# Stores on ScalarE's queue, later turns and a last item summed by quarter, in the last product of a layer on one core

## The chip, the cores and the metric

The kernel runs on one core of a Trainium2 chip. The metric is the time of one execution on the device in microseconds (us). The core has a matrix engine (TensorE, PE in the profile, with its weight loads as PEld), three engines for elementwise work (VectorE is DVE, ScalarE is ACT, GpSimd is POOL), and SyncE (SP), which here only starts transfers. Each engine works through its own instructions in order. A transfer (DMA) is started by an instruction in the queue of one of these engines, and such an instruction waits, like any other, until what it needs is ready; what is behind it on that engine waits too.

## What is computed

The inputs are 4 sequences of 512 tokens with 1024 features, all in float32.

```python
xn = layernorm(x)                                     # x: (4, 512, 1024)
qkv = xn @ w_qkv                                      # 32 query heads, 8 key/value heads of 128
scores = einsum('bqhgd,bkhd->bhgqk', q, k) * scale
attn = softmax(scores - slopes * sqrt(distance), causal)
a = einsum('bhgqk,bkhd->bqhgd', attn, v).reshape(4, 512, 4096)
out = x + a @ w_o + (xn @ W.T + b) + lora(xn)         # lora: one of four ranks per token
```

The last line is one product in the kernel: the 1024 features of xn and the 4096 of a are contracted together (5120 rows of weights, W above w_o), and the low-rank term and the bias come in as a further product over 65 rows. Its result is 2048 tokens by 1024 features, to which x is added.

## The kernel before

**Stages.** A first stage normalises x and projects it to q, k and v (to about 1150 us of the profiled execution), a second one does the attention (to about 1880 us), and the function finish does the last product (from about 1950 us to the end). Only finish is touched.

**The last product.** It is done with seven products in place of eight at each of three levels (the Winograd form of Strassen's scheme). The outer level is the index i, taken in the order OUTER = (1, 2, 6, 5, 3, 7, 4); the middle level is m, in the order MIDDLE = (1, 2, 3, 6, 7, 4, 5); one pair (i, m) is an item, and there are 49 items. The inner level is class Inner: seven products of five matmuls each (KB = 5 blocks of 128 rows; 128x128 weights against 256 tokens), in seven methods m1, m5, m6, m3, m2, m7, m4. Results stand transposed, features on partitions and tokens along them.

**The loop.** The loop at the end of finish runs an item's methods and calls beside(n, slot) after each, with slots 1 to 7; the method m4 of the item before (prev.m4) runs between slots 2 and 3. So a slot, or step, is one inner product on TensorE. In beside stand the operand sums of the next item, tokens(k) on VectorE and weights(k) on GpSimd, and the loads of the item after next (L1167 for tokens, tiles sa; L1173 to L1182 for weights, tile w). All are in a fixed order on their engines: the calls are wrapped in pin, which keeps program order, and TensorE's order is the program's.

**PSUM and its readers.** Each inner product lands in a bank of the kinds c, d or a. Where an item has a base (a tile that its result is added to), VectorE reads the bank (L128, tiles m, x, u and the like). Where it has none, which are the items with m = 1 or m = 5 and two with m = 3, ScalarE copies it (L166). The accumulation that follows in the same bank waits for that read.

**Sums and stores.** When an item's last quarter is there, after(row, col) adds whole tiles of 128x1024 elements, mostly on GpSimd, and calls done(at, t) of class Outer. What done does depends on i. For i = 1, 6 and 5 the tile goes to a scratch tensor c_d named u, w or v, with a store on SP's queue (L1387), and is loaded again later (taken, L1367) as the base of a later i. For i = 7 GpSimd adds the tile to y and v; y is stored on SP's queue (L1393), and v is a result and leaves. For i = 2, 3 and 4 the tile is a result and leaves.

**Leaving.** leave(t, where) loads the matching rows of x into a tile x_t (L1346, SP's queue, two transfers of 256 KB) and appends two turns to the queue leaving, one for each pair of sequences p. A turn does four transposes on TensorE (L1352, tile ptr_f), adds x on VectorE (128x512) and stores the result on SP's queue (L1355). A slot of 5 or later takes one turn from the queue. The x tile has four buffers, so a load of x rows waits for the store that used its buffer before.

**The end.** The last item is (4, 5). Its after adds the whole tile x_5 to y for the quarter (0, 1) on VectorE, then u and y to it on GpSimd for the quarter (1, 1); each sum leaves in two turns, which are emptied after the loop.

Of the kernel before, what the change touches and what calls it, by code (L numbers as in the profile page):

```python
# [65 lines left out]
def kernel(  # L66
# [13 lines left out]
    nc = tc.nc  # L80
# [5 lines left out]
    NP = B // 2  # L86
# [5 lines left out]
    xf = x.rearrange("b (t p) h -> p (b t) h", p=P)  # L92
    outf = out.rearrange("b (t p) h -> p (b t) h", p=P)
# [16 lines left out]
    def scratch(name, shape):  # L110
        return dram.tile(shape, F32, tag=name, name=name)
# [10 lines left out]
    c_d = {  # L122
        (n, r, c): scratch(f"c{n}_{r}{c}", [P, 2, NP, HS])
        for n in ("u", "w", "v", "y") for r in range(2) for c in range(2)
    }

    def add(eng, dst, u, v):
        return eng.tensor_tensor(dst, u, v, ALU.add)  # L128
# [1020 lines left out]
    order = [(i, m) for i in OUTER for m in MIDDLE]  # L1149
    pin = tc.keep_in_program_order  # L1150
# [126 lines left out]
    def finish(sb, homes, ops, begun):  # L1277
        bank_of = rotation(c=(3, 0), d=(2, 4), a=(5, 1), tr=(6, 7))

        def bank(kind, name):  # L1280
            t = bank_of(kind, name)
            return t if kind == "tr" else t[:, :HS]
# [4 lines left out]
        def r4(name, tag="r4"):  # L1287
            return sb.tile([P, 2, NP, HS], F32, tag=tag, name=name, bufs={"r4": 8, "u": 2}[tag])

        def quarter(t, row, col):  # L1290
            return t[:, col, row]
# [12 lines left out]
        def of(n):  # L1304
            if n not in ops:
                ops[n] = Operands(n, homes)
            return ops[n]
# [25 lines left out]
                pin(sub(nc.gpsimd, w[:, :, 2], w[:, :, 0], w[:, :, 1]))  # L1333


        leaving = deque()

        def rows(t, p, row, col, r, c):
            at = (2 * p + row) * NT + 2 * r
            return t[:, at : at + 2, ds(col * S + c * HS, HS)]  # L1340

        def leave(t, where):
            n = "_".join(str(k) for k in where)
            x_t = sb.tile([P, NP, 2, HS], F32, tag="x", name=f"x_{n}", bufs=4)
            for p in range(NP):
                nc.sync.dma_start(out=x_t[:, p], in_=rows(xf, p, *where))  # L1346

            def turn(p):
                tr = bank("tr", f"f_{n}_{p}").rearrange("p (a b k) -> p a b k", a=2, b=2)
                for k in range(2):  # L1350
                    for j in range(2):
                        nc.tensor.transpose(tr[:, k, j], t[:, j, p, ts(k, P)], ident)  # L1352
                y = x_t[:, p].rearrange("p a (b k) -> p a b k", b=2)
                pin(add(nc.vector, y, tr, y))
                nc.sync.dma_start(out=rows(outf, p, *where), in_=x_t[:, p])  # L1355

            for p in range(NP):
                leaving.append(lambda p=p: turn(p))


        BASE = {2: "u", 6: "u", 5: "w", 3: "v", 4: "y"}
        KEPT = {1: "u", 6: "w", 5: "v"}
        PLACE = {2: (0, 0), 3: (0, 1), 4: (1, 0)}
# [6 lines left out]
        class Outer:  # L1370
# [13 lines left out]
            def done(self, at, t):  # L1384
                i = self.i
                if i in KEPT:
                    pin(nc.sync.dma_start(out=c_d[(KEPT[i], *at)], in_=t))  # L1387
                elif i in PLACE:
                    leave(t, (*PLACE[i], *at))
                else:  # L1390
                    y, v = self.given.pop(at)
                    pin(add(nc.gpsimd, y, y, t))
                    pin(nc.sync.dma_start(out=c_d[("y", *at)], in_=y))  # L1393
                    pin(add(nc.gpsimd, v, v, t))
                    leave(v, (1, 1, *at))

        def item(n, outer):
            i, m = order[n]
            name = f"{i}_{m}"
            o = ops[n]  # L1400
            t = outer.t
            has = outer.base is not None
            base = None
            if m == 1:
                dst = t["u"] = r4(f"u_{i}", "u")
            elif m in (6, 7):
                dst = base = t["u"]
            elif m == 3 and has:
                dst = base = outer.given.pop((0, 1))
            else:  # L1410
                dst = r4(f"x_{name}")
                if m in (2, 4):
                    base = t["u"]
            t[m] = dst
            left = [4]

            def after(row, col):
                left[0] -= 1
                if left[0]:
                    return  # L1420
                if m in (2, 4):
                    at = {2: (0, 0), 4: (1, 0)}[m]
                    if has:
                        pin(add(nc.gpsimd, dst, dst, outer.given.pop(at)))
                    outer.done(at, dst)
                elif m == 6:
                    pin(add(nc.gpsimd, t[3], t[3], dst))
                elif m == 5:
                    pin(add(nc.vector, t[3], t[3], dst))
                    outer.done((0, 1), t[3])  # L1430
                    pin(add(nc.gpsimd, dst, dst, t["u"]))
                    if has:
                        pin(add(nc.gpsimd, dst, dst, outer.given.pop((1, 1))))
                    outer.done((1, 1), dst)

            def into(row, col):
                return quarter(dst, row, col)

            def base_of(row, col):
                return quarter(base, row, col)  # L1440

            if n == 0:
                return Plain(name, bank, o, into, None, after, begun)

            def mult(l, bk, start):
                if i in RANKED and m in RANKED and l in RANKED:
                    (_, _), (r, c), (p, d) = RANKED[i], RANKED[m], RANKED[l]
                    nc.tensor.matmul(
                        bk, low["w"][:, c, d], low["u"][:, p, ts(r, HS)], start=start, stop=False,
                        skip_group_check=True,  # L1450
                    )
                    start = False
                for _ in o.steps(l, bk, start):
                    pass

            return Inner(name, bank, tmp, mult, into, base_of if base is not None else None, after)

        def beside(n, slot):

            if n + 1 < len(order):  # L1460
                nxt = of(n + 1)
                {1: lambda: n and (nxt.tokens(1), nxt.weights(1)), 2: lambda: (nxt.tokens(2), n and nxt.weights(2)),
                 3: lambda: nxt.weights(3), 4: lambda: (nxt.tokens(4), nxt.weights(4)),
                 5: lambda: nxt.tokens(3)}.get(slot, lambda: None)()
            if n + 2 < len(order):
                o = of(n + 2)
                {2: lambda: o.load(1, 0), 3: lambda: (o.load(1, 1), o.load_weights()),
                 4: lambda: o.load(0, 0), 6: lambda: o.load(0, 1)}.get(slot, lambda: None)()
            if leaving and slot >= 5:
                leaving.popleft()()  # L1470

        outers = {}
        prev = None
        for n, (i, m) in enumerate(order):
            if m == 1:
                outers[i] = Outer(i)
                if i in RANKED:
                    low_rank(i)
            if n + 1 < len(order) and order[n + 1][1] != 1:
                outers[i].prefetch(order[n + 1][1])  # L1480
            it = item(n, outers[i])
            it.m1()
            beside(n, 1)
            it.m5()
            beside(n, 2)
            if prev is not None:
                prev.m4()
            beside(n, 3)
            for slot, step in ((4, it.m6), (5, it.m3), (6, it.m2), (7, it.m7)):
                step()  # L1490
                beside(n, slot)
            prev = it
        prev.m4()
        while leaving:
            leaving.popleft()()

    psum = ctx.enter_context(pool("psum", space=bass.MemoryType.PSUM))
    homes, begun = [], {}
# [41 lines left out]
    with tc.manual_schedule(engines={PE}):  # L1540
        with pool("c1") as home:
            homes.append(home)
            lay(home, "x")
            next(attention, None)
            with pool("c2") as sb:
                homes.append(sb)
                finish(sb, homes, ops, begun)
# [35 lines left out]
```

## Time and profile before

| what | value |
|---|---|
| median of 3 runs | 2747.62 us (2742.18 to 2752.84) |
| the profiled execution's own time | 2745.72 us |
| its span, first to last instruction | 2743.9 us |
| busy in the span: PE, DVE, ACT, POOL | 2623.8, 1772.3, 651.2, 1939.4 us |
| last product, 1952 to 2744 us: PE, DVE, ACT, POOL busy | 764.4, 473.3, 22.8, 475.6 us of 792 |
| DMA in the last product | 0.78 of the 16 engines, 275 GB/s |
| x rows, issue to landing | 5.5 / 6.7 / 10.9 us (min, median, max; 32 loads) |
| output stores, issue to landing | 2.2 / 3.8 / 5.4 us (32 stores) |
| scratch stores, issue to landing | 2.9 / 3.0 / 3.0 us |

How to read it. The times are those of one profiled execution. Busy time leaves out the instructions that issue transfers; they are listed as SPq or ACTq, the engine's sequencer. PE, DVE and the others overlap, so an idle engine costs nothing unless TensorE, or the end of the kernel, waits for it. DMA share is the mean busy share of the core's 16 DMA engines. L128, L131 and L166 are lines of small helpers (add, sub, Inner.read), so groups are told apart by the names of their tiles: t<-w are weight sums, s<-sa token sums, x, u, v, w and y result tiles.

### The profile page before, as it was taken

To read this page: it belongs to the slowest core of one execution; us is meant where nothing else is said; L and a number is where in the kernel's file an instruction comes from. 1 tells how busy PE (TensorE), PEld (TensorE's weight loads), DVE (VectorE), ACT (ScalarE), POOL (GpSimd) and SP (SyncE) were. 2 spreads that over 40 slices of the span, in tenths; PEclk is the share of its full clock that TensorE was granted. 3 is DMA by queue.
4 is the path that set the end of the run, shared out by engine and by line. 5 is a ranking of instruction groups with operands and counts; after the bars stand their busy time and mean duration, and the time that the engine had idled before them with its cause. 6 is when DMAs were issued, how large, how long until landed. Compare 5 with 4: busy or idle time off the path is not lost.

```text
span 2743.9 us, 35857 instructions
## 1 busy us (share of the span) xinstructions
PE 2623.8 (96%) x11872; PEld 2089.3 (76%) x11872; DVE 1772.3 (65%) x3620; ACT 651.2 (24%) x1727; POOL 1939.4 (71%) x1999
## 2 busy tenths in 40 slices
PE   7899999997999999999999999998799999999998
PEld 6688888886888888866666666666688888888887
DVE  6766675666667667566666666675456667566553
ACT  3001111100000000176666666663000000000000
POOL 2688877887898888667777777776465667656563
PEclk9899999999999999999999999999899999999999
DMA  3289776754966767326666666767788878788883
GB/s 135 85 297 339 258 247 203 268 186 157 345 230 232 255 216 249 138 101 217 203 218 202 219 202 220 245 220 247 271 287 308 295 289 328 234 299 302 295 292 114
DMA packets 377098, 648.06 MB, mean 236 GB/s; under 512 B 22057, under 2 KB 280489, under 8 KB 367698
## 3 DMA queue, kind: packets, MB, share of 16 engines
q1 hardware_dynamic: 324594, 583.51, 61.7%
q10 hardware_dynamic: 51040, 57.68, 6.7%
q0 software_dynamic: 1280, 4.59, 0.4%
q8 instruction: 95, 1.56, 0.2%
q14 instruction: 89, 0.73, 0.1%
HBM read 387.74 MB, written 257.96 MB: 235 GB/s over the span
## 4 chain that ended last, share of the span: by engine, by line
PE 60%; DMA 6%; POOL 4%; DVE 3%; issue 2%; SPq 0%; POOLq 0%; ACT 0%; ACTq 0%; DVEq 0%
PE pc L1228 12%; PE psc L980 10%; PE po L1018 10%; PE pc_q L549 6%; PE pd L1228 5%; PE ptr L1005 3%; PE pd_q L549 3%; PE pa L1228 3%; PE pc_kv L549 3%; DMA sa<-s 1%; PE pa_q L549 1%; PE pd_kv L549 1%; DMA w<-in_w_o_dram 1%; DMA s<-ot 1%; DVE pt L1008 1%
## 5 line engine op out<-in xcount | busy, mean ns | idle before, releaser
L994 POOL TENSOR_SCALAR p<-p,tot 128x256 f32<-128x256 f32 (+3 forms) x512 | 317.9, 642 | 134.4 <-DVE tot L992 81.3
L985 DVE CUSTOM_DVE_ANT_0 p<-psc,bias 128x256 f32<-128x256 f32 (+3 forms) x512 | 245.1, 491 | 95.6 <-PE psc L980 72.6
L980 PE MATMUL psc<-k,q 128*128 128x512 f32 (+3 forms) x1024 | 305.3, 437 | 1.3 <-ACT r_q L166 0.5
L989 ACT ACTIVATE p<-p,low 128x256 f32<-128x256 f32 (+3 forms) x512 | 283.8, 555 | 71.0 <-DVE low L985 53.6
L131 POOL TENSOR_TENSOR t<-w 128x640 f32<-128x640 f32 x96 | 181.9, 1895 | 154.6 <-DMA w<-m 62.6
L1018 PE MATMUL po<-pt,v 128*128 128x512 f32 x640 | 290.6, 592 | 0.0
L980 PEld LDWEIGHTS psc<-k,q 128*128 128x128 f32 x1024 | 172.8, 190 | 99.6 <-issue 55.5
L131 POOL TENSOR_TENSOR t<-w,t 128x640 f32<-128x640 f32 x96 | 199.4, 2077 | 51.5 <-PE pc L1228 47.7
L1005 PEld LDWEIGHTS ptr<-ident,p 128*128 128x128 f32 x1280 | 147.3, 141 | 73.2 <-issue 39.4
L1018 PEld LDWEIGHTS po<-pt,v 128*128 128x128 f32 x640 | 116.8, 190 | 108.5 <-issue 99.3
L549 PE MATMUL pc_q<-x,ti_q 128*128 128x256 f32 x704 | 182.7, 382 | 11.0 <-DVE u_q L128 5.8
L131 POOL TENSOR_TENSOR wr<-wr 128x256 f32<-128x256 f32 x220 | 170.0, 775 | 25.9 <-DMA wr<-in_w_o_dram 9.7
L1008 DVE COPY pt<-ptr 128x512 f32<-128x512 f32 x192 | 129.9, 683 | 82.0 <-PE ptr L1005 80.2
L1005 PE MATMUL ptr<-ident,p 128*128 128x128 f32 x1280 | 167.7, 274 | 6.1 <-DVE pt L1008 4.7
L549 PE MATMUL pc_q<-xi,ti_q 128*128 128x256 f32 x640 | 167.8, 385 | 3.4 <-DVE q L128 2.9
L131 POOL TENSOR_TENSOR ti_q<-w_q 128x256 f32<-128x256 f32 x128 | 106.0, 828 | 86.0 <-PE pc_kv L549 45.7
L549 PEld LDWEIGHTS pc_q<-x,ti_q 128*128 128x128 f32 x704 | 133.2, 191 | 32.9 <-DVE u_q L128 7.5
L166 ACT COPY m<-pc 128x256 f32<-128x256 f32 x30 | 11.2, 372 | 594.5 <-PE pc L1228 586.3
L131 DVE TENSOR_TENSOR wr<-wr 128x256 f32<-128x256 f32 x220 | 139.0, 632 | 11.5 <-DMA wr<-in_w_o_dram 5.9
L549 PEld LDWEIGHTS pc_q<-xi,ti_q 128*128 128x128 f32 x640 | 121.0, 192 | 24.7 <-issue 5.9
L549 PE MATMUL pd_q<-xi,ti_q 128*128 128x256 f32 x448 | 116.6, 383 | 4.2 <-POOL ti_q L131 4.2
L166 ACT COPY q<-pc_q 128x256 f32<-128x256 f32 x64 | 23.8, 373 | 386.7 <-PE pc_q L549 342.1
(300 smaller groups left out, 5947.7 us busy)
## 6 DMA issues: line engine op xcount, KB each, us to landing
sa<-s SPq DMA_DIRECT2D x98, 640.0 KB, 7.7
s<-ot SPq DMA_DIRECT2D x107, 384.0 KB, 3.8
m<-wr SPq DMA_DIRECT2D x70, 512.0 KB, 4.5
w<-m SPq DMA_DIRECT2D x28, 1280.0 KB, 11.3
w_q<-in_w_qkv_dram SPq DMA_DIRECT2D x16, 2048.0 KB, 12.2
q<-q SPq DMA_DIRECT2D x32, 1024.0 KB, 6.6
s<-os SPq DMA_DIRECT2D x45, 512.0 KB, 8.8
t<-wr SPq DMA_DIRECT2D x40, 512.0 KB, 4.1
```

Of the source, the lines that this page charges most:

```text
L131: return eng.tensor_tensor(dst, u, v, ALU.subtract)
L166: nc.scalar.copy(dst, src)
L549: nc.tensor.matmul(dst, ops_w[m][:, c, :], XI[i][m][:, c, :], start=start and c == 0, stop=c == 1, skip_group_check=True,)
L980: nc.tensor.matmul(sc[:, :n], Q[u][:, g, ts(i, P)], K[u][:, :n], start=True, stop=True)
L985: nc.vector.tensor_tensor_reduce(pr[:, g], sc[:, :n], bias[p, h][:, g, S - n :], -SCALE, BIG, ALU.add, ALU.min, low,)
L989: nc.scalar.activation(pr[:, g], pr[:, g], AF.Exp, bias=low, scale=-1.0, accum_out=tot[:, g : g + 1])
L994: nc.gpsimd.tensor_scalar(pr[:, g], pr[:, g], tot[:, g : g + 1], 1.0, ALU.mult, ALU.mult)
L1005: nc.tensor.transpose(tr[:, ts(g, P)], PR[u, i][:, g, ts(j, P)], ident)
L1008: nc.vector.tensor_copy(pt, tr)
L1018: nc.tensor.matmul(po, V[u][:, j, :], PT[i, j], start=(j == 0), stop=(j == i))
L1228: nc.tensor.matmul(bk, w[:, k], x[:, k], start=start and k == 0, stop=stop and k == KB - 1, skip_group_check=True,)
```

## The change

It touches finish alone, in three ways.

First, all stores of the last product, and its loads of x rows, are issued on ScalarE's queue, each wrapped in pin. A store is put in a list with the step at which it may go: three steps behind its sum for the scratch tensors, one step behind its turn for the output. The x rows go at the next call of beside. The counter now counts steps, and send(), called in each beside, issues what is due.

Second, a turn waits for a step instead of a slot: three steps behind done for i = 2, 3 and 4, five for i = 7. One turn is still taken per step, in order.

Third, the last item's sums are made by quarter. When its first quarter is read, y is added to u on GpSimd; each quarter of the last product is then added to t[3] on VectorE and to u on GpSimd (on VectorE for the last quarter) as it comes. The four turns of the two sums get steps of their own. A quarter with row p is one pair of sequences, so the turns with p = 0 need the first two quarters only.

```diff
-        leaving = deque()
+        leaving, stored, now = deque(), [], [0]
+
+        def send():
+            for s in [s for s in stored if s[0] <= now[0]]:
+                stored.remove(s)
+                s[1]()
+
+        def store(dst, src, wait=3):
+            stored.append((
+                now[0] + wait, lambda: pin(nc.scalar.dma_start(out=dst, in_=src))
+            ))
...
-        def leave(t, where):
+        def leave(t, where, wait=None):
...
-            for p in range(NP):
-                nc.sync.dma_start(out=x_t[:, p], in_=rows(xf, p, *where))
+
+            def arrive():
+                for p in range(NP):
+                    pin(nc.scalar.dma_start(out=x_t[:, p], in_=rows(xf, p, *where)))
+
+            stored.append((now[0], arrive))
...
-                nc.sync.dma_start(out=rows(outf, p, *where), in_=x_t[:, p])
-
+                store(rows(outf, p, *where), x_t[:, p], 1)
+
+            if wait is None:
+                return turn
             for p in range(NP):
-                leaving.append(lambda p=p: turn(p))
+                leaving.append((now[0] + wait, lambda p=p: turn(p)))
...
                 if i in KEPT:
-                    pin(nc.sync.dma_start(out=c_d[(KEPT[i], *at)], in_=t))
+                    store(c_d[(KEPT[i], *at)], t)
                 elif i in PLACE:
-                    leave(t, (*PLACE[i], *at))
+                    leave(t, (*PLACE[i], *at), 3)
...
-                    pin(nc.sync.dma_start(out=c_d[("y", *at)], in_=y))
+                    store(c_d[("y", *at)], y)
                     pin(add(nc.gpsimd, v, v, t))
-                    leave(v, (1, 1, *at))
+                    leave(v, (1, 1, *at), 5)
...
+            final = n == len(order) - 1
 
             def after(row, col):
                 left[0] -= 1
+                if final:
+
+                    if left[0] == 3:
+                        u = t["u"]
+                        pin(add(nc.gpsimd, u, u, outer.given.pop((1, 1))))
+                        turns = [leave(t[3], (*PLACE[i], 0, 1)), leave(u, (*PLACE[i], 1, 1))]
+                        for w, p, f in ((3, 0, 0), (4, 0, 1), (4, 1, 0), (4, 1, 1)):
+                            leaving.append((now[0] + w, lambda p=p, f=turns[f]: f(p)))
+                    q = quarter(dst, row, col)
+                    for acc, eng in ((t[3], nc.vector), (t["u"], nc.gpsimd if left[0] else nc.vector)):
+                        a = quarter(acc, row, col)
+                        pin(add(eng, a, a, q))
+                    return
                 if left[0]:
                     return
...
-            if leaving and slot >= 5:
-                leaving.popleft()()
+            now[0] += 1
+            send()
+            if leaving and leaving[0][0] <= now[0]:
+                leaving.popleft()[1]()
...
         prev.m4()
-        while leaving:
-            leaving.popleft()()
+        while leaving or stored:
+            now[0] += 9
+            send()
+            if leaving:
+                leaving.popleft()[1]()
```

## The prediction, made before the changed kernel was run

> **What bounds the kernel now.** I read the page first: TensorE is busy for 2623.8 us of the span of 2743.9 us (96%), so what can be won lies where it is not. Second, the busy times by stretch. The last product runs from 1952 us to the end; up to 2728 us it holds TensorE for 758.65 of 776.00 us, at a granted clock of 0.98, with the DMA engines at 0.79.
>
> ```profile
> 1952.00:2728.00 776.00, 758.65 (x3510) 662.49 (x3510) 468.96 (x487) 22.46 (x59) 470.95 (x223) 0.98 0.79 279
> ```
>
> (Columns: stretch, its length, busy PE, PEld, DVE, ACT, POOL with counts, clock, DMA share, GB/s.) So 17.35 us of idle TensorE lie in it. Third, TensorE's timeline of that stretch, which shows where. The bracket is the idle time before a group and what ended it:
>
> ```profile
> 2058.22 0.85 PE L1448 MATMUL pc<-um,lw 65*128 65x256 f32 x2 [3.65 <-DVE m L128]
> 2387.79 1.22 PE L1448 MATMUL pd<-um,lw 65*128 65x256 f32 x2 [4.09 <-DVE m L128]
> 2388.80 4.47 PE L1228 MATMUL pd<-s,w 128*128 128x256 f32 x10
> 2529.17 0.66 PE L1352 MATMUL ptr_f<-ident,v 128*128 128x128 f32 x4 [1.74 <-POOL v L128]
> 2597.59 0.83 PE L1352 MATMUL ptr_f<-ident,v 128*128 128x128 f32 x4 [2.11 <-POOL v L128]
> 2620.08 1.11 PE L1352 MATMUL ptr_f<-ident,v 128*128 128x128 f32 x4 [4.60 <-POOL v L128]
> 2620.98 4.43 PE L1228 MATMUL pa<-sa,w 128*128 128x256 f32 x10
> ```
>
> There are two kinds. In the first, VectorE released TensorE late (with two gaps near 2280 and one at 2396.58: 3.65 + 0.23 + 0.21 + 4.09 + 0.71 = 8.89 us). In the second, the transposes of a finished tile waited for its sum on GpSimd (1.74 + 2.11 + 4.60 = 8.45 us). The reader sees also that the ten matmuls behind a gap took 4.47 or 4.43 us; 2.32 is the usual figure. Why VectorE was late is in the chain of waits:
>
> ```profile
> 2373.49 3.54 POOL x L128
> 2377.10 3.50 POOL x L128
> 2381.03 0.38 SPq L1167
> 2381.46 0.78 SPq L1181
> 2382.29 0.52 SPq L1182
> 2382.86 11.75 DMA sa<-s
> 2394.70 1.49 DVE s L131
> ```
>
> GpSimd sums a tile, SP then stores it (L1387), and only behind that store can SP issue the loads of the item after next; they land 11.75 us later and VectorE, which needs them in its order, had stood still. Fourth, SP's own waits from 1950 to 2730 us (total, times, longest):
>
> ```profile
> SPq L1355 <- DVE x L128: 92.4, 18, 31.4
> SPq L1387 <- POOL x L128: 56.7, 7, 12.7
> SPq L1387 <- DVE x L128: 35.0, 3, 23.6
> SPq L1393 <- POOL w L128: 19.7, 4, 7.9
> ```
>
> Last, the end, from the timeline:
>
> ```profile
> 2731.28 0.37 ACT L166 COPY x<-pc 128x256 f32<-128x256 f32 x1 [9.91 <-PE pc L1228]
> 2731.68 1.23 DVE L128 TENSOR_TENSOR y<-y,x 128x1024 f32<-128x1024 f32 x1 [2.97 <-ACT x L166]
> 2732.99 2.35 POOL L128 TENSOR_TENSOR x<-x,u 128x1024 f32<-128x1024 f32 x1 [11.36 <-DVE y L128]
> 2735.42 2.34 POOL L128 TENSOR_TENSOR x<-x,y 128x1024 f32<-128x1024 f32 x1
> 2739.82 0.69 DVE L128 TENSOR_TENSOR x<-ptr_f,x 128x512 f32<-128x512 f32 x1 [0.16 <-PE ptr_f L1352]
> ```
>
> After the last matmul of the product (done near 2731.2) come a copy, a whole-tile add, two GpSimd adds in a row, transposes, an add, and 3.4 us from the last add's end (2740.5) to the span's end.
>
> **Part 1: stores and x rows leave SP's queue.** Moved to ScalarE's are 16 stores of sums, 32 output stores and 32 loads of x rows (80 issues: the built program has 80 fewer on SP, 80 more on ScalarE). What remains on SP in this stage are loads. No sum stands ahead of the loads of sa and w any more, so the first kind of gap should go: 8.89 us. With it goes the slow clock behind it: behind 3.65 us the pair at 2058.22 took 0.85 for a usual 0.60 and the next ten 3.90 for 2.32, so 1.8; behind 4.09 us 0.6 + 2.15 and some 0.1 more, 2.9; behind the small ones 0.2. Together 4.9, so 13.8 us. I take it whole; the lower end is 0, if the loads were late for want of DMA engines (rival A).
>
> Issue cost on ScalarE: 16 x 0.32 + 32 x 0.39 + 32 x 0.46 us (SP's medians for these lines) = 32 us in a stage where ScalarE is busy 22.46 of 776. Two x loads, 0.9 us, stand ahead of a PSUM copy at most of the places, four (1.8 us) at three; the copy's reader is TensorE two steps of 2.16 us later. I cost it at nothing; without that cover it is 0.9 us at some 12 places, 11 us.
>
> The waits move too. A ScalarE store waits for its sum with the copies of the next m=1 or m=5 item behind it. The closest case before is the burst behind i=5: the sum ended at 2380.6 and the copy of u came at 2381.6, 1 us later (i=1: 2040.7 against 2047.1; i=6: 2270.1 against 2274.9). Each is in time, with the loads on SP late; I cost it at nothing, and the other end is rival C.
>
> x rows: they were issued far ahead; now some go out with their tile, behind the copy before them. Their median to landing is 6.7 us (5.5 to 10.9). The turn of the (1,0) tiles comes three steps (6.5 us) behind, that of the (0,1) tiles two to three (4.3 to 6.5). So five or six adds on VectorE may wait 0 to 6 us each; VectorE is busy 469 of 776 us and TensorE is a bank ahead of it. Between 0 and 12 us I take 3.
>
> **Part 2: turns three or five steps behind.** For i = 2 and 3 the turns stay about where they were (steps 5, 6, 7 and on). For i = 7 they come at step 7 instead of 5. v of 2529.17 was two steps, over 4.3 us, short of that and was 1.74 late: gone. That of 2597.59, 2.11 late: gone. The third is a burst of five adds on GpSimd (w, v, x, w, v: 2612.95 to 2627.07). The first v (done 2620.0) is then asked for at 2620.1: pd started at 2613.16, plus three groups at 2.16 and the transposes. But the second v is asked for two groups and two transposes later, at 2624.8, and not ready before 2627.1; with three adds at 3.5 us (median of x<-x,u) instead of 2.35, at 2630.6. So 2.2 to 5.8 us of stall stay, with a clock cost as behind the others (1.8 to 2.6). From the middle, 3.5 + 2 = 5.5. Gained: 8.45 + clock (0.1 + 1.8 + 2.6 = 4.5) - 5.5 = 7.4 us.
> By the Trainium skill (TensorE: Matmul & The Clock Gate, What's actually happening) the clock halves only once a window of about 3.4 us was idle; by that rule the 2.11 us gap should have cost no clock, though it cost 1.8 here. With the rule a stall under 3.4 would be 2 us cheaper; the row decides.
>
> **Part 3: the last item by quarter.** u takes y before, and each quarter of the last product is added to both sums as it comes. From the copy's end (2731.65) stay: two adds of 0.42 (the 128x256 row), then four halves to turn, of which the first is done before the last matmuls. Three adds of 0.69 follow: 2731.65 + 0.84 + 2.07 = 2734.6; transposes lie beside them. Plus 3.4 us: 2738.0. Gained: 5.9 us. GpSimd's three quarter adds (0.78 each by the wr 128x256 row) end before the last matmuls do. Between 4 and 7.
>
> **Sum.** 13.8 + 7.4 + 5.9 - 3 = 24.1 us off the profiled execution: a span of 2719.8. That execution took 2745.72 us, 1.8 over its span and 1.9 under the median of the runs. On the median's scale: 2747.6 - 24.1 = **2723.5 us**. Own range: with no x-row charge and the smaller residual 28.6 off, with the larger residual and the smaller tail 19.3, and 5 either way for the spread of the runs: 2714 to 2733.
>
> **Rivals.** A. *The DMA engines set the pace.* The loads land late because the engines are full; freeing SP only starts them sooner into the same queue. For: their share is 0.79 over the stage and 0.95 in parts; i = 7 alone asks 37 MB (seven items of 3.84, plus w, v, y, x and out) in some 113 us, 328 GB/s, where slices reach 350 to 400. Against: at 2060 to 2100 us they moved 350 GB/s and TensorE was busy throughout, and in the chain SP waited before the load, not the load. Then part 1 gives 0: 2747.6 - 13.3 + 3 = 2737. The Trainium skill (DMA: Bandwidth & Descriptors, Issuing engines are not separate DMA queues) says that starting transfers from several engines saves only the time to initiate them; by that rule this rival holds.
> B. *x rows late*: the twelve us of part 1's upper bound: 2747.6 - 15 = 2732.5, and 2736 if two steps of TensorE go with it.
> C. *ScalarE stands at stores* (slower). Each PSUM copy of an m=1 or m=5 item behind a store holds a bank that TensorE needs two steps (4.3 us) later. Ten such stores wait on GpSimd, whose adds wait for a w load up to 9.6 us. If sums come 8 us later than in the trace, each of 14 items loses some 4 us: 56 against 27 gained, 2776. It decides from a mean of 2 us per item. Against it: the margins of 1 to 6 us above, and loads that come earlier, not later.
> D. *It does not free SP*: c tiles read back (L1367) wait on SP for a store that now goes out three steps later, and with it the loads behind. Store 3 us, read two steps behind it: about in time. If not, half of part 1 goes: 2730.5.
>
> **Chances.** Forecast 0.72, A 0.10, B 0.07, C 0.08, D 0.03. Within 0.5% (13.7 us, about what these runs can tell from no change) is 2733.9 to 2761.4. Faster: 0.72 x 0.98 + 0.3 of A + half of B and D = 0.77; slower: 0.08; same the rest, 0.15. Range: 2710 (no residual and no charge, 32.6 off, and 5 for the runs) to 2740 (A and B inside), C out.
>
> **What would show it.** Right: SP waits at no store in the last stage; no gap over 1 us with VectorE as releaser; one at a transpose of v near the change from i = 7 to 4, of 2 to 6 us; 6 to 7 us from the last matmuls of the product to the end. Wrong: TensorE waiting for ScalarE's copies (C), VectorE's adds on x waiting for DMA (B), sa loads as long as before and VectorE waiting for them (A), waits of SP at L1367's line (D).

## The result, and the profile after

| | before | after |
|---|---|---|
| median of the runs compared on one chip | 2744.9 us (2740.7 to 2752.8, 4 runs) | 2719.8 us (2718.1 to 2720.5, 4 runs) |
| ratio, 95% interval | | 0.9906 [0.9893, 0.9919] |
| profiled execution: own time, span | 2745.72, 2743.9 us | 2720.48, 2718.7 us |
| last product, first matmul to end of span | 1951.73 to 2743.9: 792.2 us | 1952.31 to 2718.7: 766.4 us |

The kernel is 0.9% faster, and the forecast of 2723.5 us was 3.7 us too high. Of these, 2.7 lie in its base: it started from a median of 2747.6 us, and the runs before that are compared here have 2744.9. In the profiled executions the last product is 25.8 us shorter. Its stretch up to the last matmul of a product, in the columns of the table by stretch shown of before:

```profile
1952.00:2711.95 759.95, 753.15 (x3526) 660.87 (x3527) 464.50 (x493) 22.48 (x59) 471.31 (x227) 1.00 0.80 285
```

TensorE is idle for 6.8 us of it (17.35 before), at a clock of 1.00 (0.98 before); the DMA share is 0.80 (0.79 before). TensorE's timeline after, all gaps of over 0.6 us and the group behind the last:

```profile
2159.53 0.65 PE L1368 MATMUL ptr_f<-ident,x 128*128 128x128 f32 x4 [0.91 <-DVE x L128]
...
2602.90 0.66 PE L1368 MATMUL ptr_f<-ident,v 128*128 128x128 f32 x4 [2.62 <-POOL v L128]
...
2611.20 1.12 PE L1368 MATMUL ptr_f<-ident,v 128*128 128x128 f32 x4 [2.88 <-POOL v L128]
2612.11 3.58 PE L1228 MATMUL pc<-sa11x,t 128*128 128x256 f32 x10
```

No product behind the stage's first waits for VectorE any more. At v there are two gaps, 8.3 us apart, where one was predicted, and only the second has slow matmuls behind it (1.12 for 0.60 and 3.58 for 2.32 us). The waits of SP's queue in the last product (what it waited for: us in total, times, longest):

```profile
SPq L1167 <- PE pc L1228: 340.3, 82, 24.3
SPq L1167 <- PE pa L1228: 224.2, 44, 6.4
...
SPq L1385 <- DMA cy<-w: 10.9, 2, 6.0
```

SP waits at its loads for buffers that TensorE frees, which is ahead of need, and at no store. The stores' and x rows' waits are now ScalarE's:

```profile
ACT u L166 <- DMA out_dram<-x: 16.3, 1, 16.3
ACT x L166 <- DMA out_dram<-x: 15.1, 1, 15.1
```

Two of ScalarE's copies came after some 15 us without a copy, which the profile puts down to output stores. Ahead of the first of these copies, at 2165.47, stand four output stores that ScalarE issued from 2153.79 on (11.64 us, most of it waiting). What the stores waited for are their sums: VectorE's add for the last of them (2164.34, 0.68 us) ended 0.45 us before the copy. The copy came 1.1 us after its product, and no gap of TensorE is put down to ScalarE. The end, from the timeline:

```profile
2712.00 0.37 ACT L166 COPY x<-pc 128x256 f32<-128x256 f32 x1 [9.87 <-PE pc L1228]
...
2712.74 0.42 DVE L128 TENSOR_TENSOR u<-u,x 128x256 f32<-128x256 f32 x1
...
2714.51 0.69 DVE L128 TENSOR_TENSOR x<-ptr_f,x 128x512 f32<-128x512 f32 x1 [0.15 <-PE ptr_f L1368]
```

From the last product's end (2711.95) to the end of the span it is 6.75 us, against 12.7 before.

### The profile page after: what moved, and what is told of

Its sections match the earlier page's. It is cut to its first block, busy times and chain, and to the rows that moved or that the text cites. A ratio compares the mean times of both kernels' runs of the same rounds, so it can differ in the third digit from the quotient of the medians.

```text
span 2718.7 us, 35919 instructions
## 1 busy us (share of the span) xinstructions
PE 2613.4 (96%) x11872; PEld 2083.0 (77%) x11872; DVE 1766.2 (65%) x3624; ACT 651.5 (24%) x1727; POOL 1935.3 (71%) x2001
## 4 chain that ended last, share of the span: by engine, by line
PE 66%; POOL 3%; DVE 3%; DMA 3%; issue 1%; SPq 0%; ACT 0%; ACTq 0%; DVEq 0%; POOLq 0%
PE pc L1228 14%; PE psc L980 10%; PE po L1018 10%; PE pd L1228 7%; PE pc_q L549 6%; PE ptr L1005 4%; PE pa L1228 3%; PE pd_q L549 3%; PE pc_kv L549 3%; PE pa_q L549 2%; PE pd_kv L549 1%; DMA s<-ot 1%; DVE pt L1008 1%; DVE p L985 1%; PE pa_kv L549 1%
## 5 line engine op out<-in xcount | busy, mean ns | idle before, releaser
L131 POOL TENSOR_TENSOR t<-w,t 128x640 f32<-128x640 f32 x96 | 193.8, 2019 | 54.4 <-PE pc L1228 50.7
```

Of the source, the lines that this page charges most:

```text
L131: return eng.tensor_tensor(dst, u, v, ALU.subtract)
```

## The experiments

All have the changed kernel as their base. The code ahead of the last product is the same in all of them, yet the last product began between 1946.5 and 1954.2 us in the profiled executions, which is spread that the totals carry. So each is judged by the length of the last product in its profiled execution (first matmul to end of span; one execution each), and the total stands beside it. A length still carries chance: the first ten matmuls alone took between 4.02 and 4.64 us, and the slow matmuls behind a gap differ between executions. Lengths 1 or 2 us apart are therefore told apart only where the timelines show a gap that differs.

| run | median, us | ratio to before | last product: start, length |
|---|---|---|---|
| changed kernel | 2719.8 | 0.9906 [0.9893, 0.9919] | 1952.3, 766.4 |
| e1, stores and x rows on SP | 2718.6 | 0.9900 [0.9885, 0.9915] | 1952.7, 764.8 |
| e2, v turned three steps behind | 2722.9 | 0.9918 [0.9902, 0.9935] | 1949.4, 770.9 |
| e3, last item whole | 2720.3 | 0.9909 [0.9893, 0.9926] | 1946.5, 773.5 |
| e4, scratch stores not delayed | 2720.3 | 0.9904 [0.9887, 0.9921] | 1947.2, 765.7 |
| e5, v turned eight steps behind | 2712.3 | 0.9885 [0.9867, 0.9903] | 1947.6, 763.3 |
| e6, on SP and not delayed | 2732.8 | 0.9952 [0.9936, 0.9968] | 1951.2, 780.6 |
| e7, part 1 alone | 2727.9 | 0.9938 [0.9920, 0.9956] | 1948.4, 776.8 |
| e8, eight steps and an add moved | 2712.8 | 0.9883 [0.9864, 0.9901] | 1953.1, 760.8 |
| e9, e8 and results turned four behind | 2713.8 | 0.9886 [0.9869, 0.9902] | 1954.2, 759.2 |
| e10, the add moved alone | 2715.2 | 0.9895 [0.9880, 0.9910] | 1949.6, 763.8 |

**e1. The queue alone undone.** Delays stay; the queue is SP's again.

```diff
-                now[0] + wait, lambda: pin(nc.scalar.dma_start(out=dst, in_=src))
+                now[0] + wait, lambda: pin(nc.sync.dma_start(out=dst, in_=src))
...
-                    pin(nc.scalar.dma_start(out=x_t[:, p], in_=rows(xf, p, *where)))
+                    pin(nc.sync.dma_start(out=x_t[:, p], in_=rows(xf, p, *where)))
```

> The changed kernel (span 2718.7 us) with its stores and x rows issued on SP's queue again, at the same steps, three behind the sums and one behind the turns. If it is the queue that frees the loads, SP stands at stores once more: gaps of TensorE with VectorE as releaser come back for half or all of the 13.8 us, a span of 2726 to 2733. If it is the three steps that do it, the sums are mostly done when SP comes to their stores (the burst behind i = 1 ended 8.7 us behind its last product, three steps are 6.5 us) and the span stays within 3 us, 2718 to 2722.

Measured: 764.8 us, no worse than the changed kernel. The waits of SP's queue, to be held against those of before (L1355, L1387 and L1393 there):

```profile
SPq L1347 <- POOL x L128: 22.6, 7, 6.8
SPq L1347 <- DVE x L128: 13.8, 16, 2.6
...
SPq L1347 <- POOL w L128: 10.5, 4, 7.9
```

SP still stands at stores, at the longest 6.8 us where it was 12.7 for GpSimd's x, and 2.6 where it was 23.6 (L1387) for VectorE's. (The 31.4 us at L1355 before is a wait behind the stage's last load, so it held none; up to 2720 us the longest there was 6.7.) In TensorE's timeline no product behind the stage's first waits for VectorE. So the queue of its own is not needed once the stores are delayed.

**e4. The delay alone undone.** Scratch stores go at the next step, on ScalarE.

```diff
-        def store(dst, src, wait=3):
+        def store(dst, src, wait=0):
```

> The changed kernel with the scratch stores issued at the step behind their sums instead of three steps behind, still on ScalarE's queue. If ScalarE standing at a store is what the wait guards against, the second copy of each m = 1 item waits for the burst of sums behind i = 1, 6, 5 and 7 (8 to 15 us behind the last product, where TensorE needs the copy 6.5 us behind it): gaps of TensorE of 1 to 8 us at these four places, 8 to 15 us in all, a span of 2727 to 2734. If the copies have room, nothing changes: 2718 to 2720.

Measured: 765.7 us. TensorE's timeline has one wait for a ScalarE copy, and the two-gap burst at v shows as one:

```profile
2034.98 2.40 PE L1228 MATMUL pc<-sa10y,t 128*128 128x256 f32 x10 [1.32 <-ACT m L166]
...
2600.01 1.12 PE L1368 MATMUL ptr_f<-ident,v 128*128 128x128 f32 x4 [3.05 <-POOL v L128]
```

So the delay isn't needed once the stores have ScalarE's queue; stores that wait there hold copies, and that cost TensorE 1.32 us in the whole product. Rival C had taken some 4 us for each of 14 items.

**e6. Queue and delay both undone.** With later turns and the last item by quarter kept.

```diff
-            stored.append((
-                now[0] + wait, lambda: pin(nc.scalar.dma_start(out=dst, in_=src))
-            ))
+            pin(nc.sync.dma_start(out=dst, in_=src))
...
-            def arrive():
-                for p in range(NP):
-                    pin(nc.scalar.dma_start(out=x_t[:, p], in_=rows(xf, p, *where)))
-
-            stored.append((now[0], arrive))
+            for p in range(NP):
+                nc.sync.dma_start(out=x_t[:, p], in_=rows(xf, p, *where))
```

> Edit: stores issued at once behind the sum on SyncE's queue, and the rows of x loaded there at once, as before the change; later turns and the last item by quarter stay. With the queue alone undone, and with the delay of the stores alone undone, the time did not move. Theory 1 (SyncE stands at stores whose sums are not done and holds the loads behind them; the delay and the other queue each cure it alone): with both undone the gaps in which TensorE waits for a load that VectorE released come back, 8.9 us and 4.9 us of clock, stage 766.4 + 13.8 = 780 us, total about 2733. Theory 2 (these gaps came from the turns at their old steps, since the stores of the results waited at SyncE for adds that came late there, so the later turns alone cure them): stage 766 to 768, total about 2720.

Measured: 780.6 us and 2732.8 us in total, as theory 1 had it. The gaps are back, in TensorE's timeline:

```profile
2056.69 0.70 PE L1475 MATMUL pc<-um,lw 65*128 65x256 f32 x2 [2.41 <-DVE m L128]
...
2276.76 2.43 PE L1228 MATMUL pd<-s,w 128*128 128x256 f32 x10 [1.28 <-DVE m L128]
...
2388.12 1.22 PE L1475 MATMUL pd<-um,lw 65*128 65x256 f32 x2 [4.71 <-DVE m L128]
2389.14 4.04 PE L1228 MATMUL pd<-s,w 128*128 128x256 f32 x10
```

With three of 0.20 they come to 9.0 us (8.89 before). What stands ahead of the loads, from the timeline of all engines:

```profile
2376.84 3.48 POOL L128 TENSOR_TENSOR x<-x,w 128x1024 f32<-128x1024 f32 x1
...
2380.36 0.32 SPq L1346 DMA_DIRECT2D cv<-x  x1
2380.77 0.38 SPq L1167 DMA_DIRECT2D sa11x<-s  x1
...
2386.24 1.49 DVE L128 TENSOR_TENSOR s<-sa10x,sa11x 128x1280 f32<-128x1280 f32 x1 [7.13 <-DMA sa11x<-s]
```

GpSimd's sum, the store that waits for it, and in the next instant the load of sa11x, for which VectorE stands 7.13 us. Before, it was the same load: the chain shown in the prediction ends at the sum of 2394.70, but the gap of 4.09 us at 2387.79 came behind this one, for a load issued at 2381.03 behind the same store:

```profile
2385.91 1.49 DVE L128 TENSOR_TENSOR s<-sa10x,sa11x 128x1280 f32<-128x1280 f32 x1 [6.54 <-DMA sa11x<-s]
```

With e1 and e4 this settles part 1: the load behind a store that waits is the cause, and either remedy alone takes it away.

**e7. Part 1 alone.** Turns at their old steps, last item whole.

```diff
-            if leaving and leaving[0][0] <= now[0]:
+            if leaving and slot >= 5:
...
-            final = n == len(order) - 1
+            final = False
```

> Edit: stores and rows of x on ScalarE's queue three steps (one for the results) behind their sums, as in the changed kernel; turns at their old steps and the last item summed whole, as before. It is the first part of the change alone. Theory 1 (each part is worth what its own gaps were): the stage takes 792.2 - 13.8 = 778.4 us, with no gap released by VectorE and with the gaps at turned v and at the end as before (5.95 us of end, and gaps in which TensorE waits for GpSimd's v of some 8 us). Theory 2 (turns at their old steps are what holds the loads): the stage stays at 789 to 792 us.

Measured: 776.8 us, 15.4 less than before, where 13.8 was expected. There is no gap that VectorE released until the last item; the gaps at v are as before:

```profile
2511.04 0.66 PE L1368 MATMUL ptr_f<-ident,v 128*128 128x128 f32 x4 [1.74 <-POOL v L128]
...
2581.15 0.66 PE L1368 MATMUL ptr_f<-ident,v 128*128 128x128 f32 x4 [2.11 <-POOL v L128]
...
2602.11 1.11 PE L1368 MATMUL ptr_f<-ident,v 128*128 128x128 f32 x4 [4.74 <-POOL v L128]
```

Theory 1 holds. Some 0.7 of the 1.6 us beyond the expected gain is chance: the clock behind the gaps at v cost 3.3 us here and 4.5 before, while the gaps are 0.5 us longer. The parts nearly add: 15.4 for this one and 11.6 for the two that e6 keeps (792.2 - 780.6) make 27.0, against 25.8 for all; the changed kernel's gap at the x rows, 1.0 us with its clock, is in neither.

**e2. v turned three steps behind.**

```diff
-                    leave(v, (1, 1, *at), 5)
+                    leave(v, (1, 1, *at), 3)
```

> The changed kernel with the turns of i = 7 three steps behind their sums instead of five. If the five steps took away the waits for v, those near the first and the second tile of i = 7 return (1.7 and 2.1 us, with clock 3.7) and those of the burst grow from 5.5 to 7 us or more: a span of 2723 to 2726. If those waits went only because the loads now come in time and GpSimd with them, nothing returns but the burst's: 2718 to 2721.

Measured: 770.9 us, 4.5 more than the changed kernel, and the three gaps of before are there:

```profile
2512.65 0.66 PE L1368 MATMUL ptr_f<-ident,v 128*128 128x128 f32 x4 [1.74 <-POOL v L128]
...
2581.07 0.66 PE L1368 MATMUL ptr_f<-ident,v 128*128 128x128 f32 x4 [2.10 <-POOL v L128]
...
2602.03 1.12 PE L1368 MATMUL ptr_f<-ident,v 128*128 128x128 f32 x4 [4.75 <-POOL v L128]
2602.94 4.47 PE L1228 MATMUL pa<-sa,w 128*128 128x256 f32 x10
```

They are 8.6 us against the changed kernel's 5.5; the rest is clock. Part 2's gain is the two steps that v is given. The span of 2720.3 us lies where the other reading had it (2718 to 2721), because the last product began 2.9 us earlier than in the changed kernel; the gaps are those of the first reading. The total doesn't tell the two kernels apart; the trace does.

**e3. The last item summed whole.**

```diff
-            final = n == len(order) - 1
+            final = False
```

> The changed kernel with the last item summed whole, as before: one VectorE add and two GpSimd adds of 128x1024 behind the last copy. If the end is a chain of sums, 6 us come back: from the last product's end to the span's end 12 to 13 us instead of 6.75, a span of 2724 to 2726. If the output stores or the late x rows set the end, it is the same either way: 2718 to 2720.

Measured: 773.5 us, 7.1 more, in an execution whose last product began 5.8 us earlier; so its span, 2720.0, came out where the other reading had it, and the median, 2720.3, shows nothing either. The end:

```profile
2709.05 2.35 POOL L128 TENSOR_TENSOR x<-x,u 128x1024 f32<-128x1024 f32 x1 [11.31 <-DVE y L128]
...
2711.49 2.34 POOL L128 TENSOR_TENSOR x<-x,y 128x1024 f32<-128x1024 f32 x1
...
2715.89 0.69 DVE L128 TENSOR_TENSOR x<-ptr_f,x 128x512 f32<-128x512 f32 x1 [0.16 <-PE ptr_f L1368]
```

The two whole adds on GpSimd stand in the end again, and from the last product's end (2707.35) to the span's end it is 12.65 us against 6.75: 5.9 us, which is what part 3 is worth. That the totals don't show it fits the spread of the earlier stages, whose start is on record for the profiled executions alone; a comparison of the medians of these few runs would have called part 3 worth nothing.

**e5. v turned eight steps behind.** After e2 the residual at v stood open: could the turns simply go later?

```diff
-                    leave(v, (1, 1, *at), 5)
+                    leave(v, (1, 1, *at), 8)
```

> Edit: the results of the last accumulating product (v) are turned back eight steps behind their sums instead of five; nothing else. The stage of the last product is measured from its first product to the end of the span: 766.4 us in the changed kernel. Theory (TensorE's queue stands at the first v turn of two results because GpSimd's add ends 2.6 and 2.9 us late there): three steps are some 9 us of products, more than the 2.9, so both gaps (5.50 us) and the 1.85 us of clock behind the second go, and the stage takes 766.4 - 7.4 = 759 us. Rival (what is late is moved on, not hidden: a later turn makes a later out store and a later release of the v buffer, of which there are eight, and GpSimd's late adds delay the next product's sums): gaps of the same size appear at another place, stage 764 to 767. Total time by the first: about 2712; by the rival: about 2719.

Measured: 763.3 us; the total of 2712.3 fits theory, the length lies between the two. The gaps of 2.62 and 2.88 are gone, and two smaller ones, still behind GpSimd, have come:

```profile
2610.10 0.66 PE L1368 MATMUL ptr_f<-ident,v 128*128 128x128 f32 x4 [1.30 <-POOL v L128]
...
2629.77 0.66 PE L1368 MATMUL ptr_f<-ident,x 128*128 128x128 f32 x4 [1.73 <-POOL x L128]
```

The clock behind them stayed full. What was late was partly hidden and partly moved on; GpSimd remains the one that is late.

**e10 and e8. An add of the burst moved to VectorE**, with five steps (e10) and with eight (e8).

```diff
-                    pin(add(nc.gpsimd, dst, dst, t["u"]))
+                    pin(add(nc.vector if i == 7 else nc.gpsimd, dst, dst, t["u"]))
```

> Edit: turns of v five steps behind, as in the changed kernel; alone the add of u to the item's product, for the last accumulating product, moves from GpSimd to VectorE. Stage length from its first product to the end of the span; 766.4 us in the changed kernel, 760.8 with this move and eight steps. Theory (the two gaps at v are GpSimd's queue: w, v, then this add, w, v): the move takes one add of 2.3 to 3.6 us from between the first and the second v, so the first gap (2.6 us) stays and the second (2.9 us) falls to 0 to 0.6, with the 1.85 us of slow clock behind it: stage 762 us. Rival (VectorE's or the loads' lateness sets when v is done): both gaps stay within 0.5 us, stage 766 us.

> Edit: turns of v eight steps behind, as in the run beside it, and the first of the three adds that make v (the item's product plus u, for the last accumulating product alone) on VectorE instead of GpSimd. Theory (GpSimd is what is late in that burst: its three adds of 2.35 us each stand behind weight sums): with eight steps the gaps are gone already, so nothing is gained over that run: stage 759 us. With VectorE's slack of some 100 us in the stage the add (about 1.2 us, four times) costs nothing. Rival: VectorE's adds delay its copies-with-sum for TensorE's banks, some 1.2 us gaps, at most four: stage 759 to 764.

Measured with five steps: 763.8 us, between the theory's 762 and the rival's 766.

```profile
2600.45 0.66 PE L1368 MATMUL ptr_f<-ident,v 128*128 128x128 f32 x4 [2.37 <-POOL v L128]
...
2607.58 0.66 PE L1368 MATMUL ptr_f<-ident,v 128*128 128x128 f32 x4 [1.71 <-POOL v L128]
```

The first gap stays and the second shrinks by 1.2 us instead of 2.3 or more, with no clock lost behind it. The add's place in GpSimd's queue was a cause, but its neighbours' durations were the rest: all four adds that remain took 3.3 to 3.6 us. Measured with eight steps: 760.8 us, where e5 has 763.3. I had expected no gain over e5; that was wrong, because e5 itself kept 3 us of gaps. TensorE's stretch from 1953.1 to the end of the last product's matmuls:

```profile
1953.10:2708.00 754.90, 753.21 (x3528) 660.62 (x3528) 468.33 (x495) 22.85 (x60) 471.01 (x226) 1.00 0.79 287
```

TensorE idles for 1.7 us of it. Both together show that the add's place in GpSimd's queue held the second v. The first v, 2.37 us late in e10, was held by what stands ahead of the burst (see the next section).

**e9. Results turned four steps behind**, on top of e8.

```diff
-                    leave(t, (*PLACE[i], *at), 3)
+                    leave(t, (*PLACE[i], *at), 4)
```

> Edit: v turned eight steps behind and its first add on VectorE, as in the run before this one, and the results of the other products turned four steps behind instead of three. Theory: the last gap above 0.6 us in the stage, 0.94 us at the first turned x, whose rows of x land after the turn is due, goes: stage 759.8 us against 760.8. Rival (a later turn holds its x tile, of which there are four, and the store of the result longer, so the next rows are issued later and the gap moves on): 760.8 to 763 us.

Measured: 759.2 us; the gap of 0.9 us at the first turned x is gone and none came in its place before the end, as the theory had it. In total e5, e8 and e9 can't be told apart (intervals 0.9864 to 0.9903); all lie 6 to 7.5 us under the changed kernel's 2719.8, and e9 has the shortest last product.

## Why the prediction was right, and where its steps were off

**What bounds the kernel.** Right: the last product was TensorE's, and its idle time was the two kinds of gaps. The 17.35 us of idle became 6.8, and with e8 1.7.

**Part 1, 13.8 us.** Right in size: all 8.89 us of gaps that VectorE released are gone, with their clock. By the starts of the same products in the timelines before and after (turns taken out), part 1 gave 14.6; alone it gave 15.4 (e7). The chain that was read from the profile, sum, store, load, VectorE, is the cause (e6). What the prediction put too narrowly is the remedy: it credited the gain to the stores leaving SP's queue, and leaving was not needed (e1). Costs taken as nothing held: the issues on ScalarE and the waits that moved there hid behind its 3% of use (22.48 us of 759.95) and cost 0 us of TensorE's time in the changed kernel.

**x rows, 3 us.** Mis-sized: there is one gap of 0.91 and 0.05 behind it, so 1.0 (1.1 by the products' starts). The rows did land late: issue to landing took 9.3 us at the median, where 6.7 had been assumed from before, and one VectorE add waited 4.70 us for them. But only one turn was short of it.

**Part 2, 7.4 us.** The term that was mis-sized. It gained 5.6: 13.0 us of gaps and clock before, 5.50 of gaps and 1.84 of clock left, 7.3 where I had 5.5. (By the products' starts it gained 5.8; e2 gives 4.5 for the two steps alone, with the gaps as before but 1.3 us less of clock behind them.) The stall of the second v came as predicted, 2.88 us in a range of 2.2 to 5.8. The step that failed is the sentence that the first v of the burst is in time. It took GpSimd's adds from their places in the trace of before, and these do not hold once TensorE no longer stands still ahead of them. GpSimd's timeline before:

```profile
2606.45 2.67 POOL L131 TENSOR_TENSOR t<-w,t 128x640 f32<-128x640 f32 x1
2612.95 3.52 POOL L128 TENSOR_TENSOR w<-w,x 128x1024 f32<-128x1024 f32 x1 [3.83 <-DVE x L128]
```

and after:

```profile
2593.34 2.40 POOL L131 TENSOR_TENSOR t<-w,t 128x640 f32<-128x640 f32 x1
2595.70 3.60 POOL L128 TENSOR_TENSOR w<-w,x 128x1024 f32<-128x1024 f32 x1
2599.26 3.59 POOL L128 TENSOR_TENSOR v<-v,x 128x1024 f32<-128x1024 f32 x1
2602.82 2.34 POOL L128 TENSOR_TENSOR x<-x,u 128x1024 f32<-128x1024 f32 x1
```

Before, GpSimd was idle for 3.83 us when the burst came, and began it 1.71 us after ScalarE's copy of the item's last quarter (2611.24). After, the same copy came at 2591.74 and GpSimd was still at weight sums: the burst began 3.96 us later, with no idle time ahead of it. The 2.25 us between are most of the first gap's 2.62. VectorE's add, which stands between the copy and the burst, was slower beside those weight sums (before, then after):

```profile
2611.65 1.22 DVE L128 TENSOR_TENSOR x<-x,x 128x1024 f32<-128x1024 f32 x1 [1.19 <-ACT x L166]
...
2592.14 2.20 DVE L128 TENSOR_TENSOR x<-x,x 128x1024 f32<-128x1024 f32 x1 [2.03 <-ACT x L166]
```

The lead over TensorE had been a gift of the gap of 2.11 us that the change took away. The other runs bear this out: in the three executions with that gap (before, e2, e7) the burst began 1.7 to 1.9 us after the copy, in the nine without it 2.8 to 4.9 us. Which engine is late without the gap differs. In e4 GpSimd was idle and waited for VectorE's add, and the gap at v was 3.05 us all the same (e2, then e4):

```profile
2594.90 3.53 POOL L128 TENSOR_TENSOR w<-w,x 128x1024 f32<-128x1024 f32 x1 [1.16 <-DVE x L128]
...
2592.87 3.53 POOL L128 TENSOR_TENSOR w<-w,x 128x1024 f32<-128x1024 f32 x1 [2.56 <-DVE x L128]
```

**Part 3, 5.9 us.** Right: 5.95 from the last product to the end, and 5.9 back in e3.

**Sum.** By the products' starts, 14.6 + 5.8 + 5.95 - 1.1 = 25.2 of the 25.8 us that the last product lost; 24.1 was predicted. The other 0.6 lies in the first matmuls of the stage, which the change doesn't touch (the first ten took 4.63 us before and 4.17 after). That the total is so near is partly luck: two errors cancel, 1.9 us charged too much for the x rows and 1.6 credited too much to part 2.

**The rivals.** A (the DMA engines set the pace) is refuted. VectorE's waits for sa loads fell from 40.7 us to 12.4 at the same DMA share, though the loads took as long from issue to landing (7.7 us at the median before, 7.8 after). Before, then after (total, times, longest):

```profile
DVE s L131 <- DMA sa<-s: 40.7, 12, 7.0
...
DVE s L131 <- DMA sa<-s: 12.4, 6, 2.9
```

The Trainium skill (DMA: Bandwidth & Descriptors, Issuing engines are not separate DMA queues) says that issuing from several engines saves only the time to initiate a transfer. Where the stores are delayed, e1 agrees: 764.8 against 766.4 us with another queue. Where the scratch stores are not delayed, the runs differ from it: e4, on ScalarE's queue, is 14.9 us shorter than e6, on SP's, and what e6 shows is SP's wait for late sums with the loads behind it.

B (x rows late): one gap of 0.91 us, not several. C (ScalarE stands at stores): it stood, over four stores that took 11.6 us, with a copy 1.1 us behind its product at the end of it and no gap of TensorE behind it; even with no delay it cost 1.32 us (e4). D (SP held by read-back): SP waited 10.9 us for c tiles in the largest such group, and no product waited for it.

## What to carry to other kernels

A transfer that must wait for a sum holds every later transfer of its queue; look for loads right behind such stores, and either give the stores another queue or issue them a few steps later: here each alone was worth all of it. When a gap is taken out, redo the timing of what stood idle in it: the engine that was comfortably early by the old trace was early because another stood still. And where the stages ahead vary by more than an edit is worth, compare the length of the edited stage in the trace, not the totals.

## What the runs showed of the hardware

**The price of a gap in clock is not set by its length alone.** Behind the gap of 2.11 us at v the clock cost 1.8 us before and nothing in e7 (2.11 there, too; ten matmuls at 2.32 behind it). The granted clock over the 5 us around its end was 0.66 before (2597 to 2602 us) and 1.00 in e7 (2581 to 2586). Behind 1.74 us it cost nothing before and in e2, and 1.7 in e7. In the changed kernel 2.62 cost 0.06 and 2.88 cost 1.78. The Trainium skill (TensorE: Matmul & The Clock Gate, What's actually happening) says that the window in which activity is judged runs freely, about 3.4 us long, and doesn't start with the kernel; that the same gap costs now nothing and now 1.8 us agrees with it. That the clock halves only after a whole idle window, as the prediction cites it, does not agree: every gap named here is shorter than 3.4 us.

**GpSimd's add of 128x1024 takes 2.34 us alone and 3.6 beside VectorE's sums, and one stands while the other runs.** In the changed kernel the add of 2602.82 took 2.34 us while VectorE had only an add out of a PSUM bank; the two before it took 3.60 and 3.59 beside sums of two SBUF tiles. e5's timeline shows how:

```profile
2599.23 1.48 DVE L128 TENSOR_TENSOR s<-sa10z,sa11z 128x1280 f32<-128x1280 f32 x1
2599.24 3.69 POOL L128 TENSOR_TENSOR x<-x,u 128x1024 f32<-128x1024 f32 x1
...
2601.39 2.88 DVE L131 TENSOR_TENSOR s<-s,sa 128x1280 f32<-128x1280 f32 x1
```

VectorE began 0.01 us ahead and took 1.48; GpSimd took that and its own 2.34 (3.82, recorded as 3.69). VectorE's next sum began inside it and ended at 2604.27, 1.34 us behind GpSimd's end at 2602.93. The Trainium skill (SBUF — State Buffer, Who interferes with whom) says that a VectorE instruction with two inputs in SBUF contends with a GpSimd instruction that reads SBUF, and calls the ports that they share an exclusive lock; the rows agree. That e10 gained less than the time of one add fits this: its four remaining adds took 3.33 to 3.60 us.
